# A 2-byte adjacency aggregation rewritten as one Strassen level, with its scalings on ScalarE and the repeat in the other arm of a branch

## The chip, the cores and the metric

The kernel runs on one core of one Trainium2 chip. TensorE multiplies matrices into PSUM, VectorE and ScalarE work element by element and read PSUM, GpSimd works element by element in SBUF and issues some DMAs, and SyncE (SP) issues the rest. Each engine runs its own instructions in order, and a semaphore wait holds all that stands behind it on that engine. The metric is device time in microseconds (us), the median of several runs.

## The reference

`x` has 3327 rows of 512, `adj` is a 3327 x 3327 matrix of zeros and ones (about 1% ones). Layer 0 is two attention layers with a residual and a norm; layer 1 is a binary graph layer, and its last two lines are what the change is about:

```python
def _gat_layer(x, W, adj):
    proj = x @ W
    Wh, Ws = jnp.split(proj, 2, axis=-1)
    a = jax.nn.softmax(Wh @ Ws.T, axis=-1) * adj
    return jax.nn.leaky_relu(a @ Wh + x, 0.01)
# layer 0
h = x
for l in range(2):
    h = _gat_layer(h, W_stack[l], adj)
x = _layernorm(x + h)
# layer 1: signs of the weights, positive signs of x
xw = (x > 0) @ sign(weight).T
x = _layernorm(x + relu(adj @ xw))
```

`xw` holds whole numbers of at most 512 in size, so `adj @ xw` can be multiplied with both operands in 2-byte floats without loss.

## The kernel before

Rows are cut into 26 tiles of 128 (the last has 127) and 13 groups of two tiles; a group is named g, a pair of tiles on the contracted side q or p. For each attention layer `project` makes the projections, and `attention` runs 169 steps (g, q). In a step TensorE makes scores some 30 steps ahead, VectorE and ScalarE make the softmax, `masked` multiplies by the adjacency pair (loaded by `load_adj`), `sums` makes Strassen's left sums on GpSimd, and `values` multiplies by one level of Strassen's scheme in fp32, with its right sums loaded as `ws`. The order of every engine inside a step is written by hand: each piece carries a position, and the pieces of a step are emitted sorted by it.

In the second layer two more things happen beside the steps. `halved` copies each adjacency pair to 2 bytes on GpSimd and stores it in DRAM (`adj_d`), and `exact` counts, on VectorE, the entries that the 2-byte copy changed. `finish` ends a group: residual, statistics (`mv`), sign, and the product `xw` (L781), which goes to DRAM as 2-byte numbers (`xw_d`) and is loaded again by `load_products`.

The aggregation then needs, for output tile t, 26 matmuls of 128 x 128 by 128 x 512 in 2-byte floats (`aggregate`, L896), one for each tile j. Adjacency comes in slabs of four tiles (`load_aggregate`, L883), seven slabs a group, into the ring of 33 slots called "s". The first 66 matmuls fill TensorE while group 12 finishes its attention; `finale` runs the others group by group. After a tile's 26 matmuls `norm_out` loads `h` (L115), standardizes it (L907), adds the rectified sum (L910), takes the moments (L912, L914), and scales (L916 on ScalarE, L917 and L919 on VectorE); the store goes out on GpSimd's queue. `finale` stands outside the hand-ordered part: there the framework's scheduler orders the instructions.

At the very end the count is reduced to one flag (L939 to L945), each engine loads it (L946), and a branch (L947) skips a repeat of the aggregation in fp32 unless an entry was not exact.

Of the kernel before, what the change touches and what calls it, by code (L numbers as in the profile page):

```python
# [9 lines left out]
F32 = mybir.dt.float32  # L10
# [9 lines left out]
P = 128  # L20
# [9 lines left out]
def kernel(  # L30
# [18 lines left out]
    def rows(t):  # L49
        return min(P, N - t * P)  # L50
# [360 lines left out]
    def attention(l, att):  # L411
# [199 lines left out]
        def halved(g, q):  # L611

            _, n = half_cols(g)
            at = adj[g, q]
            ah = att.tile([P, 2, HW], F16, tag="adj_h", bufs=2, name=f"ah_{g}_{q}")
            adj[g, q, "h"] = ah
            to = adj_d[g]
            if rows(2 * q + 1) == P:
                nc.gpsimd.tensor_copy(ah[:, :, :n], at[:, :, :n])
                nc.gpsimd.dma_start(out=to[:, 2 * q : 2 * q + 2, :n], in_=ah[:, :, :n])  # L620
                return
            for a in range(2):
                j = 2 * q + a
                r = rows(j)
                nc.gpsimd.tensor_copy(ah[:r, a, :n], at[:r, a, :n])
                load_rows(nc.gpsimd, to[:, j, :n], ah[:, a, :n], r)

        def exact(g, q):

            _, n = half_cols(g)  # L630
            at, ah = adj.pop((g, q)), adj.pop((g, q, "h"))
            junk = att.tile([P, 2, HW], U8, tag="junk", bufs=1, name=f"junk_{g}_{q}")
            i = g * NQ + q
            if rows(2 * q + 1) == P:
                nc.vector.scalar_tensor_tensor(
                    junk[:, :, :n], ah[:, :, :n], 1.0, at[:, :, :n], ALU.mult, ALU.not_equal,
                    accum_out=cnt[:, i : i + 1],
                )
                return
            both = small.tile([P, 2], F32, tag="both", name=f"both_{g}")  # L640
            nc.vector.memset(both, 0.0)
            for a in range(2):
                r = rows(2 * q + a)
                nc.vector.scalar_tensor_tensor(
                    junk[:r, a, :n], ah[:r, a, :n], 1.0, at[:r, a, :n],
                    ALU.mult, ALU.not_equal, accum_out=both[:r, a : a + 1],
                )
            nc.vector.reduce_sum(cnt[:, i : i + 1], both, axis=AX.X)

# [189 lines left out]
                do()  # L839
            return  # L840

        fill = [(0, j, i) for j in range(EARLY) for i in range(2)]
        fill += [(1, j, 0) for j in range(EARLY)]
        for n, do in zip((2, 8, 26, 4, 6, 6, 6, 4, 4), later):
            do()
            for g, j, i in fill[:n]:
                aggregate(g, j, i)
            fill = fill[n:]
        for g, j, i in fill:
            aggregate(g, j, i)  # L850


    JL = 4
    EARLY = NT - 4
    XH = NT // 2
    xw, xw_tiles, ah, po = {}, [], {}, {}

    def load_products(v):


        first = NQ * (NQ - 3), NQ * NQ - 16
        if v in first:
            xh = ops.tile([P, XH, D], F16, tag="gs", name=f"xw_{len(xw_tiles)}")
            xw_tiles.append(xh)
            for a in range(XH):
                xw[len(xw)] = xh[:, a]
        for t in range(2 * NQ - 2):
            g, i = divmod(t, 2)
            made = (g + 1) * NQ - 1 + (5, 9)[i]
            if v == max(made + 1, first[t // XH] + t % XH):  # L870
                nc.sync.dma_start(out=xw[t], in_=xw_d[t])
        g, j0 = divmod(v - first[1], -(-NT // JL))
        if 0 <= g < 2:
            load_aggregate(g, [j0 * JL])

    def load_aggregate(g, parts=range(0, NT, JL)):
        _, n = half_cols(g)
        for j0 in parts:
            t = slot([P, JL, HW], F16, f"ahl_{g}_{j0}")
            js = range(j0, min(NT, j0 + JL))  # L880
            full = [j for j in js if rows(j) == P]
            if full:
                nc.sync.dma_start(  # L883
                    out=t[:, : len(full), :n], in_=adj_d[g, :, j0 : j0 + len(full), :n]
                )
            for j in js:
                if rows(j) < P:
                    load_rows(nc.sync, t[:, j - j0, :n], adj_d[g, :, j, :n], rows(j))
                ah[g, j] = t[:, j - j0]

    def aggregate(g, j, i):
        t = 2 * g + i
        if j == 0:
            pool, tag = (ps_ch, "ch") if (g, i) < (1, 1) else (ps_acc, "acc")
            po[t] = pool.tile([P, D], F32, tag=tag, name=f"agg_{t}")
        nc.tensor.matmul(  # L896
            po[t][: rows(t)], ah[g, j][: rows(j), i * P : i * P + rows(t)],
            xw[j][: rows(j)], start=(j == 0), stop=(j == NT - 1),
        )

    def norm_out(t, po, tag):
        r = rows(t)
        span = slice(t * P, t * P + r)
        h = ring.tile([P, D], F32, tag="h", name=f"ho{tag}_{t}")
        load_rows(nc.sync, h, h_d[span, :], r)
        h = h[:r]
        nc.vector.tensor_scalar(  # L907
            h, h, mv[:r, t, 0:1], rstd[:r, t : t + 1], ALU.subtract, ALU.mult
        )
        nc.vector.scalar_tensor_tensor(h, po[:r], 0.0, h, ALU.max, ALU.add)  # L910
        st = small.tile([P, 6], F32, tag="bn", name=f"bo{tag}_{t}")
        nc.vector.bn_stats(st[:r], h)  # L912
        m2 = small.tile([P, 2], F32, tag="mv2", name=f"mo{tag}_{t}")
        nc.vector.bn_aggr(m2[:r], st[:r])  # L914
        rs = small.tile([P, 1], F32, tag="rs", name=f"rs{tag}_{t}")
        nc.scalar.activation(rs[:r], m2[:r, 1:2], AF.Sqrt, bias=eps[:r])  # L916
        nc.vector.reciprocal(rs[:r], rs[:r])  # L917
        o = ring.tile([P, D], F32, tag="xr", name=f"out{tag}_{t}")
        nc.vector.tensor_scalar(  # L919
            o[:r], h, m2[:r, 0:1], rs[:r], ALU.subtract, ALU.mult  # L920
        )
        load_rows(nc.gpsimd, out[span, :], o, r)

    def finale():
        nc.scalar.activation(rstd, mv[:, :, 1], AF.Sqrt, bias=eps)
        nc.vector.reciprocal(rstd, rstd)
        for g in range(NQ):
            if g > 1:
                load_aggregate(g)
            for j in range(NT):  # L930
                for i in range(2):
                    if j >= EARLY or (g, i) >= (1, 1):
                        aggregate(g, j, i)
            for i in range(2):
                norm_out(2 * g + i, po[2 * g + i], "")


        bad = small.tile([P, 1], F32, tag="bad", name="bad")
        nc.vector.reduce_max(bad, cnt, axis=AX.X)  # L939
        pb = ps_tr.tile([1, P], F32, tag="tr", name="pbad")  # L940
        nc.tensor.transpose(pb, bad, ident)
        flag = small.tile([1, 1], F32, tag="flag", name="flag")
        nc.vector.reduce_max(flag, pb, axis=AX.X)
        flag_i = small.tile([1, 1], I32, tag="flag_i", name="flag_i")
        nc.vector.tensor_copy(flag_i, flag)  # L945
        inexact = nc.values_load(flag_i[0:1, 0:1], min_val=0, max_val=2 * CW)  # L946
        with tc.If(inexact > 0):  # L947
            for t in range(NT):
                r = rows(t)
                pf = ps_acc.tile([P, D], F32, tag="acc", name=f"aggf_{t}")  # L950
                for j in range(NT):
                    at = slot([P, P], F32, f"af_{t}_{j}")
                    load_rows(
                        nc.sync, at[:, :r],
                        adjT[j * P : j * P + rows(j), t * P : t * P + r], rows(j),
                    )
                    xf = slot([P, D], F32, f"xwf_{t}_{j}")
                    nc.vector.tensor_copy(xf[: rows(j)], xw[j][: rows(j)])
                    nc.tensor.matmul(
                        pf[:r], at[: rows(j), :r], xf[: rows(j)],  # L960
                        start=(j == 0), stop=(j == NT - 1),
                    )
                norm_out(t, pf, "f")

    for l in range(L):
        with tc.tile_pool(name=f"pre{l}", bufs=1, reuse_waits="tile") as pre:
            with tc.manual_schedule():
                project(l, pre)
        with tc.tile_pool(name=f"att{l}", bufs=2, reuse_waits="tile") as att:
            with tc.manual_schedule():  # L970
                attention(l, att)
            if l == L - 1:
                finale()


# [30 lines left out]
```

## Time and profile before

| what | value |
|---|---|
| time, median of 3 runs | 2721.83 us (2717.41 to 2726.82) |
| the profiled execution: time / span | 2719.29 us / 2717.4 us |
| TensorE, VectorE, ScalarE, GpSimd busy | 98%, 69%, 24%, 48% of the span |
| attention ends, aggregation alone from | about 2555 us |
| last aggregation matmul ends | about 2703 us |
| aggregation matmuls | 676 |
| DMA | 639.54 MB, mean 235 GB/s |

The times are of one profiled execution, from its first to its last instruction; the program's own time is a little longer than the span. A busy TensorE is not TensorE at its peak, since matmuls overlap; the distance between starts says what one costs. L numbers are lines of the kernel before.

### The profile page before, as it was taken

The numbers are of one execution on the slowest core, as the hardware profiler recorded it, in microseconds if no ns is written. First come the engines' busy times: TensorE is split into PE (matmuls) and PEld (weight loads), VectorE is DVE, ScalarE is ACT, GpSimd is POOL, SyncE is SP. The second block draws the span as 40 slices with busy tenths as digits, with TensorE's granted clock in tenths as the row PEclk, the third lists the DMA queues.
The fourth block names the chain that finished last, engine by engine and source line by source line (L and its number), as shares of the span: only waits on it lengthen the run. The fifth ranks groups of instructions, "written<-read, shape, count | busy, mean of one in ns | idle before, by whom it ended". The sixth has DMA issues, their size and how long they took to land.

```text
span 2717.4 us, 38059 instructions
## 1 busy us (share of the span) xinstructions
PE 2651.7 (98%) x12409; PEld 2233.5 (82%) x12409; DVE 1877.1 (69%) x3511; ACT 665.2 (24%) x1571; POOL 1313.6 (48%) x2170
## 2 busy tenths in 40 slices
PE   9999999999999999998999999999999999998997
PEld 6888888888888888876888888888888888877543
DVE  5654777777777777786664667777677777778543
ACT  2323222222222222211332322222222222222100
POOL 2450455555555555775452154545545455566401
PEclk9999999999999999999999999999999999999999
DMA  5765777676777767776665667777777777687882
GB/s 191 258 208 161 237 233 257 226 260 233 257 238 235 260 227 240 254 260 220 235 206 178 206 224 261 239 248 255 238 252 237 275 236 242 235 274 255 286 284 92
DMA packets 280817, 639.54 MB, mean 235 GB/s; under 512 B 35921, under 2 KB 128735, under 8 KB 279078
## 3 DMA queue, kind: packets, MB, share of 16 engines
q1 hardware_dynamic: 244038, 527.32, 58.7%
q0 software_dynamic: 36576, 109.73, 11.0%
q8 instruction: 102, 1.67, 0.2%
q14 instruction: 101, 0.83, 0.1%
HBM read 527.22 MB, written 109.69 MB: 234 GB/s over the span
## 4 chain that ended last, share of the span: by engine, by line
PE 85%; issue 6%; DMA 4%; POOL 3%; DVE 2%; SPq 0%; ACT 0%; POOLq 0%; DVEq 0%; ACTq 0%
PE acc L682 34%; PE pZ L441 19%; PE pY L441 10%; PE pX L441 5%; PE pZ_wh L309 3%; PE pD L441 3%; PE pZ_g L363 3%; DMA ws<-ws_d 2%; PE pY_wh L309 2%; PE pY_g L363 2%; PE pm L273 1%; PE pxw L781 1%; PE pxt L221 1%; PE pX_wh L309 1%; PE pX_g L363 1%
## 5 line engine op out<-in xcount | busy, mean ns | idle before, releaser
L441 PE MATMUL pZ<-gs,xs 128*128 128x256 f32 x2496 | 635.8, 379 | 0.0
L441 PEld LDWEIGHTS pZ<-gs,xs 128*128 128x128 f32 x2496 | 473.6, 190 | 64.8 <-ACT u L458 0.3
L655 POOL TENSOR_TENSOR as<-s 128x128 f32<-128x128 f32 x338 | 168.4, 498 | 734.1 <-DVE s L600 577.1
L682 PE MATMUL acc<-ws,s 128*128 128x256 f32 x1352 | 404.3, 381 | 0.0
L682 PE MATMUL acc<-ws,as 128*128 128x256 f32 x1352 | 352.7, 382 | 30.0 <-DMA ws<-ws_d 17.4
L682 PE MATMUL acc<-wh,s 128*128 128x256 f32 x1352 | 356.9, 380 | 1.7 <-DVE h L706 1.7
L441 PE MATMUL pY<-gs,xs 128*128 128x256 f32 x1248 | 320.3, 379 | 0.0
L511 DVE TENSOR_TENSOR top<-top,s 128x512 f32<-128x512 f32 x312 | 252.7, 810 | 97.8 <-ACT s L493 58.2
L682 PEld LDWEIGHTS acc<-ws,as 128*128 128x128 f32 x1352 | 253.6, 190 | 75.0 <-POOL as L657 12.8
L682 PEld LDWEIGHTS acc<-wh,s 128*128 128x128 f32 x1352 | 258.0, 191 | 37.5 <-DVE h L706 2.1
L682 PEld LDWEIGHTS acc<-ws,s 128*128 128x128 f32 x1352 | 257.3, 191 | 35.1 <-DVE h L714 0.2
L582 DVE TENSOR_TENSOR s<-s,off 128x512 f32<-128x512 f32 x338 | 273.0, 808 | 0.1
L483 DVE TENSOR_TENSOR s<-p,u 128x256 f32<-128x256 f32 x156 | 67.5, 433 | 286.2 <-ACT u L458 285.3
L441 PEld LDWEIGHTS pY<-gs,xs 128*128 128x128 f32 x1248 | 237.0, 190 | 32.3
L585 ACT ACTIVATE s<-s 128x512 f32<-128x512 f32 x338 | 213.7, 632 | 201.5 <-DVE s L582 200.5
L593 DVE TENSOR_TENSOR total<-total,s 128x512 f32<-128x512 f32 x312 | 259.3, 831 | 0.8 <-ACT s L585 0.8
L657 POOL TENSOR_TENSOR as<-s 128x128 f32<-128x128 f32 x338 | 236.5, 700 | 26.5
L600 DVE TENSOR_TENSOR s<-s,adj 128x512 f32<-128x512 f32 (+1 forms) x312 | 226.1, 725 | 5.7
L458 ACT COPY u<-pZ 128x256 f32<-128x256 f32 x312 | 116.4, 373 | 459.9 <-PE pZ L441 459.9
L656 POOL TENSOR_TENSOR s<-s 128x128 f32<-128x128 f32 x338 | 215.2, 637 | 26.5
L658 POOL TENSOR_TENSOR as<-s,as 128x128 f32<-128x128 f32 x338 | 210.5, 623 | 26.5
L682 PE MATMUL acc<-wh,as 128*128 128x256 f32 x676 | 205.8, 386 | 0.0
(185 smaller groups left out, 3501.1 us busy)
## 6 DMA issues: line engine op xcount, KB each, us to landing
ws<-ws_d SPq DMA_DIRECT2D x338, 512.0 KB, 3.9
xs<-xs_d SPq DMA_DIRECT2D x182, 512.0 KB, 5.9
adj<-in_adjT_dram SPq DMA_DIRECT2D x288, 256.0 KB, 4.4
xs<-xs_d SPq DMA_DIRECT2D x156, 384.0 KB, 6.3
gs_d<-gsp POOLq DMA_DIRECT2D x88, 256.0 KB, 3.2
gs<-gs_d SPq DMA_DIRECT2D x12, 1792.0 KB, 11.0
adj_d<-ah POOLq DMA_DIRECT2D x144, 128.0 KB, 4.4
ahl<-adj_d SPq DMA_DIRECT2D x72, 256.0 KB, 4.4
```

The costliest lines, as they stand in the source:

```text
L309: nc.tensor.matmul(bank, of[LEFT[i]][:, k], wr[RIGHT[i]][:, k], start=(start and k == 0), stop=(k == 1), skip_group_check=True,)
L441: nc.tensor.matmul(ch[bank], xs[c, q, a][:, k], gs[c][:, b, k], start=(start and k == 0), stop=(k == 1), skip_group_check=True,)
L511: nc.vector.tensor_tensor(top[i], top[i], t, ALU.max)
L582: nc.vector.tensor_tensor(s, s, off[g].to_broadcast([P, 2, HW]), ALU.subtract)
L585: nc.scalar.activation(sc[g, q], sc[g, q], AF.Exp)
L593: nc.vector.tensor_tensor(total[g], total[g], sc[g, q], ALU.add)
L600: nc.vector.tensor_tensor(s[:, :, :n], s[:, :, :n], at[:, :, :n], ALU.mult)
L655: nc.gpsimd.tensor_tensor(s3, a11, a21, ALU.subtract)
L656: nc.gpsimd.tensor_tensor(a21, a21, a22, ALU.add)
L657: nc.gpsimd.tensor_tensor(s2, a21, a11, ALU.subtract)
L658: nc.gpsimd.tensor_tensor(s4, a12, s2, ALU.subtract)
L682: nc.tensor.matmul(acc[g][i // 2][:, i % 2], a[i], b[i], start=(q == 0 and i % 2 == 0), stop=(q == NQ - 1), skip_group_check=True,)
```

## The change

- **Aggregation.** A group's two output tiles are made together by one level of Strassen's scheme: seven products of 128 x 128 by 128 x 256 for each pair p of 13, so 91 matmuls a group in place of 52 twice as wide. Products lie two to a PSUM bank, (0, 1), (2, 3), (4, 5), (6), and the banks are worked one after the other, each over all 13 pairs. Groups alternate between two sets of four banks.
- **Sums.** `product_sums` makes four right sums for each pair on VectorE (44 of 52 operations in the last row of the attention), in the space of `wh`. `adjacency_sums` makes four left sums a slab: s1 and s2 on VectorE, s3 on GpSimd, s4 on VectorE for groups 0 and 1 and on GpSimd from group 2 on. Each slab and its sums take a slot of the ring "s". The padded last tile is filled with zeros by memsets on GpSimd.
- **Loads.** The slabs of groups 0 and 1 are loaded every second step of the last 27 or so steps, not every step of the last 16. Those of group g+1 are loaded while group g runs.
- **Output.** `take_out` adds the products from PSUM; `standard` standardizes `h` on ScalarE in two operations; `moments` as before; `scaled` scales on ScalarE in two operations, on VectorE in the last group. The store goes out on SP's queue. `h` now lies in the four buffers "adj", two a group.
- **Order.** `finale` stands in the hand-ordered part; all its pieces have positions.
- **Exactness.** `exact` compares `adj` with (`adj` > 0) and no longer reads the 2-byte copy. The flag is made in group 11; the branch's first arm holds the last group's output, the other arm the repeat.

```diff
@@ exact
-                    junk[:, :, :n], ah[:, :, :n], 1.0, at[:, :, :n], ALU.mult, ALU.not_equal,
+                    junk[:, :, :n], at[:, :, :n], 0.0, at[:, :, :n], ALU.is_gt, ALU.not_equal,
...
@@ end of attention
-        fill = [(0, j, i) for j in range(EARLY) for i in range(2)]
-        fill += [(1, j, 0) for j in range(EARLY)]
-        for n, do in zip((2, 8, 26, 4, 6, 6, 6, 4, 4), later):
+        fill = [
+            (g, b, p, i) for g in range(2) for b in range(3) for p in range(EARLY)
+            for i in BANKS[b]
+        ]
+        for n, do in zip((4, 16, 48, 8, 12, 12, 12, 8, 8), later):
...
+        finale(att)
-    EARLY = NT - 4
+    NS = -(-NT // JL)
+    EARLY = NQ - 2
+    BANKS = (0, 1), (2, 3), (4, 5), (6,)
...
@@ load_products
+        p = v - NQ * (NQ - 1) - 2
+        if 0 <= p < EARLY:
+            product_sums(p)
+        n, odd = divmod(v - NQ * NQ + 4 * NS - 1, 2)
+        if odd:
+            return
+        if 0 <= n < 2 * NS:
+            load_aggregate(*divmod(n, NS))
+        if 0 <= n - 1 < 2 * NS - 1:
+            adjacency_sums(*divmod(n - 1, NS))
+
+    def product_sums(p):
+        x1, x2 = xw[2 * p], xw[2 * p + 1]
+        xt[p] = wh[p].bitcast(F16).rearrange("p a n -> p (a n)")[:, : 4 * HD].rearrange(
+            "p (i n) -> p i n", i=4
+        )
+        right_sums(x1[:, :HD], x1[:, HD:], x2[:, :HD], x2[:, HD:], *(xt[p][:, i] for i in range(4)))
...
+    def adjacency_sums(g, s):
+        n = min(JL, NT - s * JL) // 2
+        a = ah[g, s].rearrange("p (b k) (i c) -> p b k i c", k=2, i=2)[:, :n]
+        a11, a21, a12, a22 = (a[:, :, k, i] for k in range(2) for i in range(2))
+        t = slot([P, 4, 2, P], F16, f"asm_{g}_{s}")
+        s1, s2, s3, s4 = (t[:, i, :n] for i in range(4))
+        nc.gpsimd.tensor_tensor(s3, a11, a21, ALU.subtract)
+        nc.vector.tensor_tensor(s1, a21, a22, ALU.add)
+        nc.vector.tensor_tensor(s2, s1, a11, ALU.subtract)
+        (nc.vector if g < 2 else nc.gpsimd).tensor_tensor(s4, a12, s2, ALU.subtract)
...
+    def aggregate(g, b, p, i):
+        if p == 0 and i == BANKS[b][0]:
+            pool, tag = (ps_acc, "acc") if g % 2 else (ps_ch, "ch") if b < 3 else (ps_tr, "tr")
+            po[g, b] = pool.tile([P, 2, HD], F32, tag=tag, name=f"agg_{g}_{b}")
...
+        nc.tensor.matmul(
+            po[g, b][:, i % 2], asm[g, p][i], of[i],
+            start=(p == 0 and i % 2 == 0), stop=(p == NQ - 1), skip_group_check=True,
+        )
...
@@ finale (norm_out and the old finale are removed)
+        def load_h(g):
+            for t in half_tiles(g):
+                h = h_of[t] = att.tile([P, D], F32, tag="adj", bufs=4, name=f"ho_{t}")
+                load_rows(nc.sync, h, h_d[t * P : t * P + rows(t), :], rows(t))
+
+        def standard(t):
...
+            nc.scalar.activation(h, h, AF.Identity, bias=nmean[:r, t : t + 1])
+            nc.scalar.activation(h, h, AF.Identity, scale=rstd[:r, t : t + 1])
...
+        def scaled(t, fast):
...
+            nc.vector.reciprocal(rs[:r, 0:1], rs[:r, 0:1])
+            if fast:
...
+            else:
+                nc.vector.tensor_scalar(rs[:r, 1:2], m2[:r, 0:1], -1.0, None, ALU.mult)
+                nc.scalar.activation(h, h, AF.Identity, bias=rs[:r, 1:2])
+                nc.scalar.activation(h, h, AF.Identity, scale=rs[:r, 0:1])
+            load_rows(nc.sync, out[t * P : t * P + r, :], h, r)
...
+        for g in range(NQ):
...
+            done = {b: (n + 1) / len(todo) for n, (b, p, i) in enumerate(todo)}
+            t1, t2 = half_tiles(g)
+            if 1 <= g and g + 1 < NQ:
+                for s in range(NS):
+                    work += [
+                        (-0.1 + s / NS, lambda s=s: load_aggregate(g + 1, s)),
+                        (0.04 + s / NS, lambda s=s: adjacency_sums(g + 1, s)),
+                    ]
+            if g + 1 < NQ:
+                work.append((0.5, lambda: load_h(g + 1)))
+            work += [(0.1, lambda: standard(t1)), (0.3, lambda: standard(t2))]
+            if g == NQ - 2:
+                work.append((0.95, check))
+            if g < NQ - 1:
+                for b in range(3):
+                    work.append((done[b] + 0.02, lambda b=b: take_out(g, b)))
+                work += [(0.98, lambda: moments(t1, c_of[g][0]))]
+            if g > 0:
+                u1, u2 = half_tiles(g - 1)
+                work += [
+                    (0.001, lambda: take_out(g - 1, 3)), (0.05, lambda: scaled(u1, False)),
+                    (0.08, lambda: moments(u2, c_of[g - 1][1])),
+                    (0.2, lambda: scaled(u2, False)),
+                ]
+            for _, do in sorted(work, key=lambda e: e[0]):
+                do()
         inexact = nc.values_load(flag_i[0:1, 0:1], min_val=0, max_val=2 * CW)
-        with tc.If(inexact > 0):
+        with tc.If(inexact < 1) as cmp:
...
+            moments(t1, c_of[g0][0])
+            scaled(t1, True)
+            take_out(g0, 3)
...
+        with cmp.Else():
```

`take_out(g, b)` is the attention's function of that name with the banks' products: for bank 0 a ScalarE copy of the first product and one VectorE sum, for bank 1 two sums, for bank 2 three, for bank 3 one.

## The prediction

> **What bounds the kernel now.** The page comes first: TensorE is busy nearly everywhere.
>
> ```profile
> span 2717.4 us, 38059 instructions
> PE 2651.7 (98%) x12409; PEld 2233.5 (82%) x12409; DVE 1877.1 (69%) x3511; ACT 665.2 (24%) x1571; POOL 1313.6 (48%) x2170
> ```
>
> 98% is an average, so I read the stage that the change rewrites, the aggregation, in the table by stretches (busy us per engine, then clock, DMA share, GB/s):
>
> ```profile
> 2510.00:2520.00 10.00, 7.83 (x32) 6.32 (x31) 8.85 (x15) 1.75 (x3) 7.92 (x12) 0.83 0.85 300
> ...
> 2555.00:2703.00 148.00, 147.85 (x691) 68.00 (x689) 70.17 (x162) 9.70 (x30) 14.96 (x27) 1.00 0.67 219
> 2703.00:2717.40 14.40, 0.00 (x0) 0.00 (x0) 3.79 (x12) 0.54 (x2) 1.61 (x3) 0.65 0.13 41
> ```
>
> From 2555 to 2703 TensorE never stops; VectorE works half the time, ScalarE 7%, GpSimd 10%. The chain of waits shows one group of 256 rows leaving every 11.2 us (2672.86 to 2684.08), which is 52 matmuls:
>
> ```profile
> 2672.86 0.54 POOL out_dram L115
> ...
> 2684.08 0.54 POOL out_dram L115
> ```
>
> So one matmul costs 11.22/52 = 0.2157 us. The groups then give the prices of operations like the new ones (mean ns after the busy time):
>
> ```profile
> L896 PE MATMUL agg<-xw,ahl 128*128 128x512 f16 x625 | 141.6, 379 | 0.0
> L585 ACT ACTIVATE s<-s 128x512 f32<-128x512 f32 x338 | 213.7, 632 | 201.5 <-DVE s L582 200.5
> L916 ACT ACTIVATE rs<-mo,eps 128x1 f32<-128x1 f32 x25 | 6.2, 288 | 128.5 <-DVE mo L914 128.5
> L714 DVE TENSOR_TENSOR h<-acc,h 128x256 f32<-128x256 f32 x26 | 10.8, 415 | 0.0
> L721 POOL TENSOR_TENSOR total<-total 128x256 f32<-128x256 f32 x26 | 19.8, 761 | 0.0
> ```
>
> and the DMA issues of 2640 to 2703, when the queues are light, the time to landing (last number, us):
>
> ```profile
> out_dram<-out POOLq DMA_DIRECT2D x11, 256.0 KB, 4.0
> ho<-h_d SPq DMA_DIRECT2D x9, 256.0 KB, 3.2
> ahl<-adj_d SPq DMA_DIRECT2D x6, 255.0 KB, 3.7
> ```
>
> Last, the timeline of the end: VectorE's last scaling starts at 2706.34 and takes 0.55; from its end to the end of the span pass 10.5 us (last stores, branch, end).
>
> **What the Trainium skill says.** (1) "TensorE: Matmul & The Clock Gate", Back-to-back issue gap: N/2.4 + 2.5 ns for a warm stream. N = 512 gives 215.8, the trace 215.7; so 256 columns cost 109 ns. Each new matmul loads its own weights; in the trace four transposes at L771, each with its own load, start 0.22 us before the next matmul, 55 ns apiece, so loads hide. (2) "VectorE: DVE Perf Modes", perf-mode tier table: two-input operations on 2-byte data run two elements a cycle. No row here shows one; with the page's (cycles + 151)/0.96 a 256-element sum is an estimated 290 ns, against 424 unpaired, near the 415 above. (3) "GPSIMD Engine Reference", Performance versus the Vector engine: about 2.6 cycles an element for two inputs. The trace's best 128- and 256-element sums, 442 and 722 ns, give 2.2 ns an element, which is that. (4) "ScalarE: Activation LUTs", What ACT_TABLE_LOAD costs: a per-partition scale or bias adds 93 ns. The trace has 632 without and 288 for one element with; so Identity on 512 elements costs an estimated 706 ns. The same page puts identity in every table set, so no table switches.
>
> **The change, part by part.**
>
> *Matmuls.* 676 x 0.2157 = 145.8 us become 13 x 13 x 7 = 1183 x 0.109 = 129.2: a gain of 16.6 us, if TensorE stays the bound. A group costs 91 x 0.109 = 9.9 us.
>
> *The count of inexact entries* reads fp32 twice instead of a 2-byte copy: same elements, same form, 690 ns either way. VectorE no longer waits for GpSimd's cast (28 us in all, hidden under TensorE except in the last row of the attention). Zero.
>
> *Sums during the last attention row (2497 to 2555).* VectorE gets 44 product sums (about 0.3 us each, 13 us) and some 20 adjacency sums (6 us) on 42 busy of 57; GpSimd 7 sums and memsets (7 us) on 43. Against that the 14 adjacency loads are spread over 27 steps instead of 14, in a stage where DMA is at 0.85 to 0.99 and TensorE waits for ws. I take +4 us (bounds -3, +10): TensorE there is fed by VectorE and GpSimd, so nothing hides an overload.
>
> *Start.* The fill hides the last group's finishing as before (132 half matmuls for 66). xw of the last tile, at 2570.8 before, comes at 2574.8; then VectorE runs four product sums (1.2), the last adjacency sums (0.7), the take-outs of group 0 (2.3), its moments with one more take-out and sum (5.4 less overlap 1.0): the second moments of group 0 end at about 2583.4. Call such an end M.
>
> *The ring of one group.* Engines run in order, and the changed order closes a ring from M (moments of t2, group g-1) to the next M:
> - ScalarE: square root, standard(t1 of g), then scaled(t2 of g-1): 0.3 + 2 x 0.7 + 2 x 0.7, with overlaps 3.05 us.
> - SP: the store of t2 now stands on SP, not GpSimd. Landing: 3.4 us (SP's 256 KB transfers show 3.2 to 3.7; the old store 4.0).
> - SP: load_h(g+1) takes over that buffer ("adj" has 4, two a group), so it waits for the landing, and behind it on SP stand slabs 5 and 6 of group g+1. 0.4 us to issue, 3.5 to land: slab 5 is there at M + 10.4.
> - VectorE reaches the sums of slab 5 at M + 7.5 and waits. Behind them stand take_out(2), the sums of slab 6, moments t1, take_out(3), the sums of slab 0 of g+2, two reciprocals, moments t2: 2 x 0.3, 3 x 0.36, 0.5, 1.65, 0.36, 0.6, 0.3, 1.65, with hand-overs and GpSimd's contention 6.2 us.
>
> Sum 16.6 us a group, against 9.9 of matmuls and 11.2 before. Eleven such turns (groups 1 to 11) take 182.6 us. TensorE waits some 5 us a turn for slabs 5 and 6. GpSimd's 14 sums (12 x 0.72 + 2 x 0.45 = 9.5, with contention up to 1.7 times that) fit inside.
>
> *End.* The check stands before the last take-outs (+0.9 in group 11, gone from the end). From the last M: ScalarE's queue and the branch 5.4, take-outs, two moments and scalings 8.0, then as before 10 us (the jump over the other arm replaces the old one).
>
> Sum: 2583.4 + 182.6 + 0.9 + 13.4 + 10.0 = 2790.3 us of span, against 2717.4. The profiled execution took 2719.3 (span + 1.9), the median of the runs is 2721.8 (2.5 above it). Carried over: 2795.
>
> **Rivals.**
> - *Ring without the store.* If slabs 5 and 6 land in time (the two landings together under 4 us instead of 6.9), the ring closes over ScalarE alone: M, 3.05, standard(t2), copy of p1 at 4.65, then VectorE's nine microseconds: 13.6 a group, 2762. For it: no SP store is in the trace, so its landing is the least known term. Against it: transfers that land in under 2 us hardly occur there, and an instruction that waits does hold SP (from 2400 to 2555 its queue stood 68 us behind loads of ws that waited for TensorE).
> - *TensorE stays the bound (faster).* If sums and stores keep ahead, TensorE ends 16.6 - 4 earlier and the end is 1.5 shorter: 2703.5, carried over 2708. It decides where a turn takes about 10 us (2790.3 - 72.9 spread over 11 turns). VectorE alone has 10 us of work a group (14 adjacency sums 3.7, take-outs 2.6, moments 3.3, small ones 0.5), so it needs every wait gone. In the trace's favour: VectorE is half idle here now.
> - *A slower ring.* Sums unpaired (424 ns: +0.8), landings as in the busy stage (4.1 and 4.3: +1.5), GpSimd's contention (its 128-element sums double from 0.45 to 0.79 beside VectorE): 19.3 a turn, 2824. GpSimd alone would bind beyond 16.6, at 1.7 times its bare time.
> - *No effect*: losses of the row and gains of the matmuls cancel: needs a turn near 10.5.
>
> **How the numbers follow.** The ring with the store 0.64, without it 0.15, the slower one 0.08, the faster case 0.09, no change 0.04. Slower 0.87, same 0.04, faster 0.09; 0.3% (8 us) is about what three runs can tell. The likeliest time is 2795; its own range is 2770 to 2820 (turns of 15 to 18.3 us, the row -3 to +10). Down to 2750 and up to 2824 the range takes in the ring without the store and part of the slower one.
>
> **What would show it.** Right: TensorE's busy share from 2600 on falls to about 0.65, with gaps once per group and a lower clock; groups leave every 16 to 17 us; SP waits for the landing of out_dram at load_h; VectorE's longest waits are for slab 5 (ahl). The first 2440 us are as before. Wrong: groups every 10 to 11 us with TensorE full; a VectorE or GpSimd that is busy throughout (then the sums are the price, not the waits); table loads on ScalarE; a last attention row that has grown by more than 10 us. The weakest terms are the two landings, which no SP store of before shows, and the 290 ns of a 2-byte sum.

## The result

The changed kernel takes 2838.86 us (median of 4 runs, 2837.61 to 2839.85), the kernel before 2719.62 us beside it: ratio 1.0435, 95% interval 1.0416 to 1.0454. Slower, as forecast, but by 119 us where 73 were forecast, and outside the range. The page of the changed kernel, then its table by stretches (busy us per engine, then clock, DMA share, GB/s):

```profile
span 2838.1 us, 39982 instructions
PE 2677.3 (94%) x12891; PEld 2298.8 (81%) x12916; DVE 1972.7 (70%) x3825; ACT 739.4 (26%) x1684; POOL 1437.3 (51%) x2332
```

```profile
2525.00:2550.00 25.00, 21.09 (x90) 16.62 (x91) 24.37 (x53) 4.13 (x8) 16.47 (x26) 0.93 0.79 254
...
2600.00:2650.00 50.00, 31.38 (x205) 22.50 (x206) 27.21 (x78) 13.74 (x24) 26.06 (x41) 0.70 0.49 156
...
2750.00:2800.00 50.00, 27.73 (x193) 20.61 (x191) 24.03 (x67) 14.39 (x26) 22.69 (x37) 0.74 0.38 121
```

From 2600 on, where TensorE was full before, it works 63% of the time at first, 73 and 68% in the two stretches left out, and 55% in the last. No engine is full in its place: VectorE and GpSimd work half the time, ScalarE a third. So the time is in waits. The first line is the last row of the attention: there VectorE is full (24.37 of 25 us). The same 25 us in the kernel before:

```profile
2525.00:2550.00 25.00, 20.65 (x94) 16.01 (x93) 17.56 (x33) 3.58 (x6) 20.41 (x32) 1.00 0.89 303
```

The timeline of VectorE gives the length of a turn. M is the end of such a line, the moments of a group's second tile:

```profile
2709.84 0.18 DVE L1000 BATCH_NORM_AGGREGATE mo<-bo 128x2 f32<-128x6 f32 x1
...
2728.22 0.18 DVE L1000 BATCH_NORM_AGGREGATE mo<-bo 128x2 f32<-128x6 f32 x1
```

From the one line to the other a turn takes 18.4 us. The eleven turns are 20.4, 18.8, 18.3, 18.7, 19.0, 19.7, 18.4, 18.6, 18.6, 21.0 and 32.2 us; the first M is at 2595.2, the last at 2818.8. Against the forecast of 2790.3 for the span:

| stretch | forecast | measured | difference |
|---|---|---|---|
| to the first M | 2583.4 | 2595.2 | +11.8 |
| nine ordinary turns | 9 x 16.6 | 9 x 18.9 | +21 |
| last two turns | 2 x 16.6 | 21.0 + 32.2 | +20 |
| flag (measured inside the last turn) | 0.9 | | -0.9 |
| from the last M to the end | 23.4 | 19.3 | -4.1 |

The sum is +48, which is 2838.1. Who waits for whom in the ordinary turns, from 2610 to 2750 (engine and line, what released it: us in all, times, longest)?

```profile
PE agg L939 <- DMA ahl<-adj_d: 43.3, 26, 3.8
DVE asm L925 <- DMA ahl<-adj_d: 30.1, 21, 3.7
...
DVE c L981 <- ACT ap L980: 27.4, 7, 3.9
```

VectorE waits for slabs of the adjacency (`ahl`) and for ScalarE's copy of the first product (`ap`, called p1 here); TensorE waits for slabs. VectorE and ScalarE wait for no matmul there, and GpSimd only twice (4.2 us in all), so TensorE's lower clock (0.70 to 0.79) is not what sets the turn. What holds up SP, which issues the loads? Its own waits in the same stretch:

```profile
SPq L115 <- ACT rs L1002: 42.2, 8, 5.3
SPq L115 <- POOL ahl L906: 37.7, 7, 5.7
...
SPq L115 <- DMA out_dram<-ho: 1.3, 6, 0.4
```

The landing of the store, a term of 3.4 us in the forecast's ring, is the last line: 1.3 us in seven turns. In its place stands L906, a memset on GpSimd that fills the padded tile of a group's last slab. It holds SP 5.4 us a time. The timelines of GpSimd and of VectorE in one turn show why, and what it costs:

```profile
2720.76 0.67 POOL L927 TENSOR_TENSOR asm<-ahl,asm 128x256 f16<-128x256 f16 x1 [0.22 <-DVE asm L926]
2721.37 0.31 POOL L906 MEMSET ahl<- 128x256 f16 x1
```

```profile
2719.72 0.29 DVE L925 TENSOR_TENSOR asm<-ahl 128x256 f16<-128x256 f16 x1 [0.69 <-DMA ahl<-adj_d]
...
2723.87 0.22 DVE L925 TENSOR_TENSOR asm<-ahl 128x128 f16<-128x128 f16 x1 [2.19 <-DMA ahl<-adj_d]
```

The memset takes 0.31 us, but it is written after the fourth sum of slab 5 in GpSimd's queue, so it can't start before slab 5 has landed and been summed. The load of slab 6's padded tile waits for the memset, and two slabs of the group after stand behind it on SP. VectorE then waits 2.19 us in front of slab 6. In the last turn every slab has such a memset, one column wide, since group 12 has 255 columns. GpSimd there:

```profile
2789.65 0.75 POOL L924 TENSOR_TENSOR asm<-ahl 128x256 f16<-128x256 f16 x1 [3.43 <-DMA ahl<-adj_d]
2790.62 0.67 POOL L927 TENSOR_TENSOR asm<-ahl,asm 128x256 f16<-128x256 f16 x1 [0.22 <-DVE asm L926]
2791.23 0.12 POOL L908 MEMSET ahl<- 128x4 f16 x1
2794.45 0.75 POOL L924 TENSOR_TENSOR asm<-ahl 128x256 f16<-128x256 f16 x1 [3.10 <-DMA ahl<-adj_d]
```

Load, sums, memset, next load: 4.8 us a slab, one after the other. That reading makes SP's queue and memsets of 0.1 to 0.3 us responsible for some 40 us. Whether it holds, only runs can tell.

### The profile page after: what moved, and what is told of

Same layout as the page of the kernel before. It is cut to its first block, busy times and chain, and to the rows that moved or that the text cites. A ratio compares the mean times of both kernels' runs of the same rounds, so it can differ in the third digit from the quotient of the medians.

```text
span 2838.1 us, 39982 instructions
## 1 busy us (share of the span) xinstructions
PE 2677.3 (94%) x12891; PEld 2298.8 (81%) x12916; DVE 1972.7 (70%) x3825; ACT 739.4 (26%) x1684; POOL 1437.3 (51%) x2332
## 4 chain that ended last, share of the span: by engine, by line
PE 82%; DMA 5%; DVE 5%; POOL 3%; issue 2%; ACT 1%; SPq 0%; POOLq 0%; DVEq 0%; ACTq 0%
PE acc L681 32%; PE pZ L441 19%; PE pY L441 9%; PE pX L441 5%; PE pZ_wh L309 3%; PE pD L441 3%; PE pZ_g L363 3%; DMA ahl<-adj_d 3%; PE agg L939 2%; DMA ws<-ws_d 2%; PE pY_wh L309 2%; PE pY_g L363 1%; PE pxt L221 1%; PE pX_wh L309 1%; PE pm L273 1%
## 5 line engine op out<-in xcount | busy, mean ns | idle before, releaser
L654 POOL TENSOR_TENSOR as<-s 128x128 f32<-128x128 f32 x338 | 168.1, 497 | 731.9 <-DVE s L600 319.2
L681 PE MATMUL acc<-ws,as 128*128 128x256 f32 x1352 | 356.9, 386 | 28.4 <-DMA ws<-ws_d 18.8
L511 DVE TENSOR_TENSOR top<-top,s 128x512 f32<-128x512 f32 x312 | 246.1, 789 | 110.3 <-ACT s L493 65.3
L655 POOL TENSOR_TENSOR s<-s 128x128 f32<-128x128 f32 x338 | 233.9, 692 | 26.5
L656 POOL TENSOR_TENSOR as<-s 128x128 f32<-128x128 f32 x338 | 221.2, 654 | 26.5
L657 POOL TENSOR_TENSOR as<-s,as 128x128 f32<-128x128 f32 x338 | 216.5, 641 | 26.5
## 6 DMA issues: line engine op xcount, KB each, us to landing
gs<-gs_d SPq DMA_DIRECT2D x12, 1792.0 KB, 11.1
```

The source lines that it names most:

```text
L511: nc.vector.tensor_tensor(top[i], top[i], t, ALU.max)
L654: nc.gpsimd.tensor_tensor(s3, a11, a21, ALU.subtract)
L655: nc.gpsimd.tensor_tensor(a21, a21, a22, ALU.add)
L656: nc.gpsimd.tensor_tensor(s2, a21, a11, ALU.subtract)
L657: nc.gpsimd.tensor_tensor(s4, a12, s2, ALU.subtract)
L681: nc.tensor.matmul(acc[g][i // 2][:, i % 2], a[i], b[i], start=(q == 0 and i % 2 == 0), stop=(q == NQ - 1), skip_group_check=True,)
```

## The experiments

Twelve kernels were timed beside the kernel before. Line numbers differ a little between them. "Mean turn" is the mean of the eleven. First M and mean turn are of one profiled execution each, whose time can lie some us off the median (pads 4.6 above it, pfo_nosums 5.9).

| kernel | median us | ratio to before (95%) | first M | mean turn |
|---|---|---|---|---|
| changed kernel | 2838.9 | 1.0435 (1.0416 to 1.0454) | 2595.2 | 20.3 |
| pads | 2797.6 | 1.0289 (1.0271 to 1.0306) | 2592.6 | 17.1 |
| first | 2785.0 | 1.0248 (1.0231 to 1.0265) | 2592.9 | 15.3 |
| pads_first | 2780.4 | 1.0228 (1.0211 to 1.0245) | 2592.1 | 15.1 |
| pads_bufs | 2801.8 | 1.0302 (1.0285 to 1.0320) | 2595.0 | 16.9 |
| order_alone | 2848.6 | 1.0478 (1.0461 to 1.0496) | 2598.5 | 21.1 |
| scale_dve | 2841.1 | 1.0453 (1.0436 to 1.0470) | 2595.0 | 20.2 |
| pf_order | 2754.6 | 1.0130 (1.0113 to 1.0147) | 2591.4 | 12.9 |
| pfo_s4 | 2762.3 | 1.0152 (1.0130 to 1.0173) | 2593.3 | 13.4 |
| pf_noxt | 2774.5 | 1.0206 (1.0189 to 1.0223) | 2588.0 | 15.1 |
| pf_noadj | 2730.6 | 1.0048 (1.0031 to 1.0066) | 2586.5 | 10.8 |
| pfo_nosums | 2718.5 | 0.9996 (0.9987 to 1.0005) | 2585.8 | 10.3 |
| exact_alone | 2723.2 | 1.0019 (1.0008 to 1.0030) | | |

### pads: the memsets out of the loads' way

```diff
@@ halved
+                if n < HW:
+                    nc.gpsimd.memset(ah[:, :, n:], 0.0)
                 nc.gpsimd.tensor_copy(ah[:, :, :n], at[:, :, :n])
-                nc.gpsimd.dma_start(out=to[:, 2 * q : 2 * q + 2, :n], in_=ah[:, :, :n])
+                nc.gpsimd.dma_start(out=to[:, 2 * q : 2 * q + 2], in_=ah)
...
@@ load_aggregate
-        if len(full) < len(js):
-            nc.gpsimd.memset(t[:, len(full) : len(js)], 0.0)
-        if n < HW:
-            nc.gpsimd.memset(t[:, : len(js), n:], 0.0)
...
+        nc.sync.dma_start(out=t[:, : len(js)], in_=adj_d[g, :, j0 : j0 + len(js)])
```

> Edit: the padding of the halved adjacency (column 255 of the last group, row 127 of the last tile) is zeroed before it is stored, during the attention, so the slab loads of the aggregation bring it along; the memsets on GpSimd and the extra load issues of the last slab are gone. Theory A (SP, in order, is held at the last slab until GpSimd has worked off its sums and reaches the memset): the nine ordinary turns fall from 18.9 us to 16.7, close to the 16.6 of the forecast, the last two from 21.0 and 32.3 to the same length; 9 x 2.2 + 4.3 + 15.6 = 40 us less, 2799 us. Theory B (the time goes to VectorE's and GpSimd's own work on the sums, and the memset only stands where SP would wait anyway): ordinary turns stay at 18 to 19, only the last two become ordinary, 16 us less, 2823 us.

Measured: 2797.6 us, 41 less. Ordinary turns are 16.5 to 18.7 us, the last two 16.7 and 17.6. Theory A holds, and with it the size: a wait of SP for GpSimd, not GpSimd's work (it has all its sums still), cost 41 of the 119 us. Two smaller things went with the memsets, and no run separates them: the extra loads for the padded tile (two a group, 0.75 us on SP in the turn above), and the last group's rows of 255 columns, whose slabs landed no later than others (2.9 us against 3.0). SP's waits in the same stretch no longer contain a memset:

```profile
SPq L115 <- ACT rs L993: 87.1, 9, 10.1
...
SPq L115 <- DMA out_dram<-ho: 1.1, 5, 0.2
```

What is left is SP's wait for ScalarE, whose scaled tile it is to store; the landing of the store is again nearly nothing.

### pads_bufs: is the landing of the store in the ring?

```diff
@@ load_h
+            if g % 2:
+                two = att.tile([P, 4, HD], F32, tag="ws", name=f"ho2_{g}")
             for t in half_tiles(g):
...
+                if g % 2:
+                    h = h_of[t] = two[:, 2 * i : 2 * i + 2].rearrange("p a n -> p (a n)")
```

> On top of pads: the h tiles of every second group lie in the buffers of ws, which is idle by then, so a load of h never waits for the landing of a store two groups back. The forecast had that landing in its ring with 3.4 us a turn: if so, turns fall from 16.8 to about 13.4, 2760 us. From the trace of pads SP stands only 1.1 to 1.5 us between the store and the load of h, and VectorE waits 0.9 us for slab 5: turns 15.9, 2788 us. If the landing is hidden: no change, 2798 us.

Measured: 2801.8 us, not less than pads. The landing is hidden: SP reaches the load of h 4.5 to 4.9 us after M with it and 4.5 to 4.6 without, because it issues two slabs between the store (M + 3.1) and that load. The third case of the expectation came true; my reading of the trace of pads, 0.9 us a turn, was also wrong.

### first and pads_first: the slabs ahead of the stores

```diff
@@ finale
-                        (-0.1 + s / NS, lambda s=s: load_aggregate(g + 1, s)),
+                        (-1.0 + 0.1 * s, lambda s=s: load_aggregate(g + 1, s)),
```

> Edit: within a group, the seven slab loads of the next group are put at the head of the list, ahead of the stores and of the loads of h on SP; memsets stay. Theory A (slabs 5 and 6 are late because SP stands at the stores, the loads of h and the memsets): VectorE does not wait for slabs any more, the ring closes over ScalarE and VectorE alone, 13.6 us a turn as worked out in the forecast's first rival: first M at 2595, 11 x 13.6, 19 us of end, 2765 us. Theory B (the sums themselves are the price): turns stay near 18, 2825 to 2839 us.

> Both edits: padding zeroed before it is stored, and the slab loads at the head of each group. Theory A: as with the slabs first alone, and up to 10 us less, since SP waits for no memset at all: 2755 to 2765 us. Theory B: 16 us below the changed kernel, 2823 us.

Measured: 2785.0 and 2780.4 us. Most of A's gain is there: VectorE waits for slabs no more (but once in first, 2.3 us), nearly all turns are 15.1 us, and with the slabs first the memsets cost little more (4.6 us, with one turn of 17.8 us, the last but one). But 13.6 us was too low. VectorE's longest wait in pads_first, from the table of waits, and ScalarE's timeline of one turn (M at 2666.63):

```profile
DVE c L972 <- ACT ap L971: 39.1, 10, 3.9
```

```profile
2666.67 0.29 ACT L993 ACTIVATE rs<-mo,eps 128x1 f32<-128x1 f32 x1
2666.87 0.71 ACT L958 ACTIVATE ho<-ho,nmean 128x512 f32<-128x512 f32 x1
2667.61 0.72 ACT L959 ACTIVATE ho<-ho,rstd 128x512 f32<-128x512 f32 x1
2668.24 0.71 ACT L1007 ACTIVATE ho<-ho,rs 128x512 f32<-128x512 f32 x1
2668.98 0.72 ACT L1008 ACTIVATE ho<-ho,rs 128x512 f32<-128x512 f32 x1
2669.61 0.71 ACT L958 ACTIVATE ho<-ho,nmean 128x512 f32<-128x512 f32 x1
2670.34 0.72 ACT L959 ACTIVATE ho<-ho,rstd 128x512 f32<-128x512 f32 x1
2670.97 0.35 ACT L971 COPY ap<-agg 128x256 f32<-128x256 f32 x1
```

The copy of p1, which VectorE needs to take the first bank out, stands behind the square root and six scalings: it ends at M + 4.7, as the forecast's first rival had it (4.65). From there VectorE needs 10.4 us to the next M, not 9: sums of 2-byte data that take 0.28 to 0.29 us alone take 0.59 to 0.66 beside GpSimd's. So the ring over ScalarE exists, behind the one over SP.

### pf_order: ScalarE's order

```diff
@@ finale
-            work += [(0.1, lambda: standard(t1)), (0.3, lambda: standard(t2))]
+            work += [(0.1, lambda: standard(t1)), (0.45, lambda: standard(t2))]
...
-                    (0.2, lambda: scaled(u2, False)),
+                    (0.32, lambda: scaled(u2, False)),
```

> On top of pads_first: the scalings of the second tile and the standardisation of the second tile stand behind the copy of p1 on ScalarE instead of ahead of it (positions 0.32 and 0.45 of a group, for 0.20 and 0.30). Theory (each turn VectorE stands 3.9 us in front of that copy, which is behind six scalings): the wait falls to about 0.9, 12.1 us a turn, 2747 us. Rival (VectorE's and GpSimd's own work, 10.8 and 9.5 us a turn with contention, takes up what is freed): 13.5 or more, 2763 us. If the wait is off the path: 2780 us.

Measured: 2754.6 us, 25.8 less; turns are 12.9 us. That is about midway between the theory (2747) and its rival (2763), and both have a share in it: VectorE's wait for the copy of p1 fell from 3.9 to 1.3 us a turn, and the sums took up part of what was freed. The table by stretches:

```profile
2600.00:2650.00 50.00, 45.27 (x365) 36.32 (x364) 43.15 (x122) 25.62 (x44) 38.08 (x56) 0.92 0.65 217
```

VectorE works 86% of the time and TensorE 91%. The waits are mostly gone and the work of the sums stands out. This is the fastest version with all of the computation that was run, and it is still 1.3% slower than the kernel before.

### order_alone: the same edit on the changed kernel

The two lines of pf_order, with memsets and slab loads where the changed kernel has them.

> On the changed kernel itself: only ScalarE's order (scalings and standardisation of the second tile behind the copy of p1), with memsets and slab loads left where they are. Theory (the slabs end last in the changed kernel's turn, the copy of p1 earlier): freed VectorE only waits longer for slab 5, and the store goes out no earlier; no gain, 2830 to 2845 us. Rival (each wait adds to the turn): the 2.2 us a turn that the same edit gave with the slabs ahead, 2815 us.

Measured: 2848.6 us, 10 more. No gain, as the theory said, but a loss just beyond what it allowed: the store of the second tile goes out at M + 4.1 instead of M + 3.1, so the slabs behind it come 1 us later, and the first nine turns are 19.7 us instead of 18.9. (3.3 of the 10 us lie ahead of the first M, which the edit hardly touches; the profiled execution was 4 us above the median.) VectorE's wait for slabs from 2610 to 2750 grew from 30.1 to 50.9 us. An edit that gives 2.2 us a turn once SP is free takes 0.8 while SP is not. It shows that SP's ring ended last, and that the store's place on SP, not its landing, is in it.

### scale_dve: the scalings of the outputs back on VectorE

```diff
-                    (0.001, lambda: take_out(g - 1, 3)), (0.05, lambda: scaled(u1, False)),
+                    (0.001, lambda: take_out(g - 1, 3)), (0.05, lambda: scaled(u1, True)),
...
-                    (0.2, lambda: scaled(u2, False)),
+                    (0.2, lambda: scaled(u2, True)),
```

> On the changed kernel itself: the scalings of the outputs back on VectorE, in one operation each; the standardisations stay on ScalarE. Theory: VectorE gets 0.8 us a turn, but the store of the second tile goes out about 1.3 us after M instead of 3.1, and with it the load of h and slabs 5 and 6 behind it: some 1 to 1.5 us less a turn, 2825 us. Rival (VectorE's work is the price): 0.8 us more a turn, 2848 us.

Measured: 2841.1 us, no change. Both were wrong; the trace shows two effects of opposite sign and like size. VectorE's timeline (M at 2709.29):

```profile
2707.20 1.15 DVE L996 SCALAR_TENSOR_TENSOR ho<-c,ho 128x512 f32<-128x512 f32 x1
...
2709.91 0.92 DVE L1011 TENSOR_SCALAR ho<-ho,mo,rs 128x512 f32<-128x512 f32 x1
```

The store does go out earlier, at M + 1.6 instead of M + 3.1. But the scaling takes 0.92 us here, against 0.546 in the kernel before, where GpSimd had next to nothing to do; and of each two L996 one takes 1.15 instead of 0.69. In the stretch before M that is 1.4 us more on VectorE, against the 1.5 us by which the store is earlier. Having the scalings on ScalarE neither cost nor gained anything in this kernel.

### pfo_s4: how much of the sums' time is disturbance

```diff
-        (nc.vector if g < 2 else nc.gpsimd).tensor_tensor(s4, a12, s2, ALU.subtract)
+        nc.vector.tensor_tensor(s4, a12, s2, ALU.subtract)
```

> On top of pf_order: the fourth adjacency sum (s4) of every slab on VectorE instead of GpSimd. VectorE gets 1.9 us of work a turn at the undisturbed 0.28 us. If the two engines disturb each other (s2 takes 0.29 us alone and 0.51 on average in pf_order), VectorE gets some 1.7 back and turns stay at 12.5 to 13, 2755 us. If VectorE's operations simply take what they take: 14.6 us a turn, 2776 us.

Measured: 2762.3 us, 7.7 more, or 0.7 a turn: nearer to the disturbance (0) than to the bare work (21 us). The groups from 2610 to 2730, in pf_order and then in pfo_s4 (busy us, mean ns of one):

```profile
L917 DVE TENSOR_TENSOR asm<-asm,ahl 128x256 f16<-128x256 f16 x56 | 28.2, 503 | 1.9
L916 DVE TENSOR_TENSOR asm<-ahl 128x256 f16<-128x256 f16 x56 | 20.5, 366 | 0.7 <-DMA ahl<-adj_d 0.7
```

```profile
L917 DVE TENSOR_TENSOR asm<-asm,ahl 128x256 f16<-128x256 f16 x54 | 18.9, 350 | 1.9
L918 DVE TENSOR_TENSOR asm<-ahl,asm 128x256 f16<-128x256 f16 x54 | 18.8, 349 | 1.8
L916 DVE TENSOR_TENSOR asm<-ahl 128x256 f16<-128x256 f16 x54 | 17.6, 326 | 0.6 <-DMA ahl<-adj_d 0.4 <-issue 0.2
```

VectorE makes half as many sums again, but the second sum falls from 503 to 350 ns. GpSimd's help with the fourth sum is worth 0.7 us a turn, not 1.9. The Trainium skill gives a reason ("SBUF — State Buffer", Who interferes with whom): a VectorE operation with two SBUF inputs contends with a GpSimd operation that reads SBUF, and so does one in a two-port mode, where whichever issues first holds the shared ports for its whole duration and the other is blocked. The trace agrees for the sums. The scaling of scale_dve also grew beside GpSimd (0.546 to 0.92 us); in which mode it runs no run shows.

### pf_noxt, pf_noadj, pfo_nosums: leaving sums out

These three leave out sums and multiply raw quarters or blocks in their place, so they don't compute the product; the number of matmuls stays.

```diff
@@ load_products (pf_noxt; pfo_nosums in product_sums itself)
-            product_sums(p)
+            xt[p] = [x1[:, :HD], x1[:, HD:], x2[:, :HD], x2[:, HD:]]
@@ adjacency_sums (pf_noadj for g > 1 only; pfo_nosums for all)
+        for b in range(n):
+            asm[g, 2 * s + b] = [e[:, b] for e in (a11, a12, a21, a22, a11, a12, a22)]
+        return
```

> On top of pads_first, left out: the 44 product sums that VectorE makes during the last row of the attention (raw quarters stand in, so part of the product is not computed). Theory (VectorE bounds that row, so its added 13 us of work come through nearly whole): the first M moves from 2592 to about 2581, 2769 us. Rival (the adjacency loads and GpSimd's sums hold the row up): at most 3 us, 2778 us.

> On top of pads_first, left out: all adjacency sums of groups 2 to 12 (raw blocks stand in, so part of the product is not computed); loads, matmuls, take-outs, moments, scalings and stores stay. If the ring over ScalarE and VectorE remains the bound: M, 4.9 us to the copy of p1, 6.2 us of take-outs and moments, 11.1 a turn, 2736 us. If only TensorE remains: 9.9 a turn, 2723 us. If the sums cost nothing on the path: 15.1 a turn, 2780 us.

> On top of pf_order, left out: every sum that the change adds, product sums and adjacency sums, in the last row of the attention and after it (raw blocks stand in, so the product is not computed). Forecast's faster rival (TensorE stays the bound): the row ends as before the change and the first M falls to about 2578, turns 10.0 us, 2578 + 110 + 20, 2709 us. If the ring over ScalarE stays at the 10.7 us of the run without adjacency sums: 2716 us. If the row does not come back (its adjacency loads are the price): 2720 us.

Measured: pf_noxt 2774.5 us, 5.9 less than pads_first, first M 4.1 us earlier (this execution was 1.5 us ahead already at 2380). That is about half of what the theory said, and more than its rival. VectorE stays full (19.5 of 20 us, twice, from 2510 to 2550) with the 44 sums gone: its other operations fill the time and take longer, a slab's three sums 0.48 to 0.54 us on average in place of 0.28 to 0.40, the count 0.97 in place of 0.76.

pf_noadj: 2730.6 us, turns of 10.8 where 11.1 and 9.9 were named. The ring over ScalarE is the bound once more (the copy of p1 is awaited 4.4 us a turn). It is still slower than before the change.

pfo_nosums: 2718.5 us, not the 2709 of the faster rival; of the two slower cases the trace supports the ring over ScalarE, since the last row did come back (see below). With every sum left out and both queues mended, the time is that of the kernel before (0.9996, 0.9987 to 1.0005). Its waits from 2600 to 2690:

```profile
DVE c L975 <- ACT ap L974: 35.9, 8, 5.6
ACT ho L961 <- DMA ho<-h_d: 19.1, 8, 3.5
```

Now h comes late, ScalarE standardizes it late, and the copy of p1 is behind that. TensorE works 98% from 2600 to 2650, but a turn is 10.3 us, not 9.9, and the first M is at 2585.8. So of the 16.6 us that the matmuls should save, nothing is left even in this form.

### exact_alone: the count on 4-byte data

The kernel before with the two lines of `exact` changed as in the diff above.

> The kernel before with one part of the change alone: the count of inexact entries reads the 4-byte tile twice instead of the 2-byte copy. Forecast: nothing, 2720 us within 0.3%. Rival: VectorE, freed of its waits for GpSimd's cast, or slowed by the wider operand, moves it by more than 8 us.

Measured: 2723.2 us, ratio 1.0019 (1.0008 to 1.0030): within 0.3%, as forecast, though not quite nothing: 5.2 us by the medians, which the changed kernel may carry too. The count runs in both attention layers, half of the pairs in each (156 operations, the first at 290 us). In the last row it takes 872 ns instead of 690, and its wait for GpSimd's cast (8.9 us ahead of six counts) is gone.

## Why the prediction was wrong

The direction was right, and so was the kind of mechanism: queues that run in order close a ring from M to M, and TensorE stands idle in it (55 to 73% busy after 2600, 65% forecast). But a link that the forecast's ring was built on, the landing of the store, is not in it, and another, the memset, was left out. The size was off in four steps.

**The ring of one group, its SP and VectorE parts.** The prediction went from the arrival of slab 5 to M in 6.2 us; in the turn above it is 8.7 (2719.72 to 2728.40). The terms that it lists for this stretch add up to 6.7 and not, hand-overs and contention included, to 6.2. The missing member is the memset ahead of slab 6, which makes VectorE wait 2.19 us: it was counted among GpSimd's work in the attention row, but not as an instruction that SP waits for and that GpSimd reaches late. With it away (pads), the kernel takes 2797.6 us against the 2795 forecast. That agreement is partly luck. The store's landing of 3.4 us that the ring contained is not in it (2.0 us, hidden: pads_bufs); VectorE's wait for the copy of p1, 3.9 us a turn, is, and stands where the forecast had a wait for slab 5 alone.

**Eleven equal turns.** The prediction multiplied one turn by eleven. The last group has 255 columns, so each of its seven slabs has a memset, and its loads go one by one: 20 us more than forecast in the last two turns, all but 1 us of it gone in pads (16.7 and 17.6). The one group that differs in shape had to be worked out by itself.

**The row of attention.** +4 us, bounds to +10; the last take-outs of that row came 13.9 us later. Part of that is older than the row: the statistics of tile 18 (`mv`), before any of the new loads and sums (the first load stands at 2436.9), are 3.6 us late in the profiled execution, here in the kernel before and in the changed one:

```profile
2378.45 0.18 DVE L763 BATCH_NORM_AGGREGATE mv<-bn 128x2 f32<-128x6 f32 x1
2382.04 0.18 DVE L762 BATCH_NORM_AGGREGATE mv<-bn 128x2 f32<-128x6 f32 x1
```

In the twelve other kernels the same statistics stand between 0.4 us earlier and 6.5 us later than before; exact_alone, which has only the new count, is 2.7 late. How much of this is the count and how much the spread of executions is not shown. From there to the last tile's statistics it takes 184.9 us in the kernel before, 195.7 in the changed one, 194.5 in pads_first, 190.4 without the product sums (pf_noxt) and 183.7 without any sum (pfo_nosums). So the row itself grew by about 10 us (10.8 in the changed kernel, 4 forecast), and all of it goes with the sums: the loads spread over more steps, which pfo_nosums keeps, cost nothing that can be seen. VectorE became the bound there, which the prediction named as a danger and then sized too low: it used 0.3 us a sum, and beside GpSimd most took 0.33 to 0.53 on average.

**End.** 4.1 us too long. Up to VectorE's last scaling, which ends at 2832.47, it was right: 13.6 us for 13.4. From there to the end of the span 5.6 us pass, where the forecast took over the 10 of the kernel before. The last stores land in 2.0 to 2.6 us on SP, and in 3.1 to 3.3 before; the rest lies behind the landing, and its cause stays open.

What held: 109 ns a matmul; 0.71 to 0.72 us a scaling on ScalarE (0.706 forecast); 0.28 to 0.29 us a 2-byte sum alone; 0.71 and 0.76 us on average for the two sums of a slab on GpSimd (0.72 forecast, before contention); the store at M + 3.1 (3.05 forecast); the first 2440 us, but for the 3.6 us above.

Of the rivals, "TensorE stays the bound" is refuted: not even pfo_nosums comes clearly under the kernel before. "Ring without the store" was right about what closes behind the SP ring, and 1.5 us short of its turn. "A slower ring" had the right direction, with GpSimd's contention as one of its causes, and the wrong main cause. "No effect" needed a turn near 10.5 us, which only pf_noadj (10.8) and pfo_nosums (10.3) come near.

The 119 us, taken apart by runs that build on one another: memsets 41, slab loads behind stores 17, ScalarE's order 26, sums 36; their total is 120. These are shares in this order of removal; order_alone shows that another order would divide them otherwise. The end point, pfo_nosums, has the cheaper matmuls and the new count, so what those save and cost is inside the 36.

## What to carry to other kernels

Follow every wait of an in-order queue to the engine that releases it, and then to what stands ahead of the releasing instruction on that engine: memsets of 0.1 to 0.3 us on the load path cost 41 us here because of their place, and zeros that were written once with the data cost nothing that could be seen. Work out the last, irregular group on its own before a turn is multiplied. And where a cheaper multiplication is bought with sums, price the sums beside what runs next to them: here the matmuls could have saved 17 us by the forecast's working, and the kernel as a whole lost that and 119 us more.

## What the hardware showed

- A 2-byte two-input sum of 256 elements on VectorE takes 0.28 to 0.29 us alone and up to 0.66 beside GpSimd's sums (pads_first); a 4-byte scaling by two per-partition values goes from 0.55 to 0.92 us (before, scale_dve). Operations that read PSUM for one input were not slowed (take-outs: 0.41 to 0.43 us in the changed kernel's last group, where GpSimd has no work, and 0.39 to 0.42 on average beside GpSimd in pf_order).
- A 256 KB store issued on SP landed in 2.0 us at the median of 2600 to 2800; on GpSimd's queue it took 4.0 before the change.
- TensorE's gaps are followed by slower matmuls. In pads_first, after 6 us in which TensorE works in short groups between waits, matmuls start 0.21 us apart up to 2666.5, then at the usual 0.11:

```profile
2665.82 0.42 PE L930 MATMUL agg<-xw,asm 128*128 128x256 f16 x1
2666.03 0.42 PE L930 MATMUL agg<-wh,asm 128*128 128x256 f16 x1
...
2666.76 0.27 PE L930 MATMUL agg<-wh,asm 128*128 128x256 f16 x1
2666.87 0.27 PE L930 MATMUL agg<-xw,asm 128*128 128x256 f16 x1
```

The Trainium skill ("TensorE: Matmul & The Clock Gate", Part 1: The HAM clock gate) has half the clock, 1.2 GHz, after an idle window of about 3.4 us; at that clock 256 columns take an estimated 213 ns, and the trace shows 0.21 us. The condition does not show here as the page puts it: the longest single wait ahead of the slow matmuls is 0.95 us. The granted clock was 0.83 from 2650 to 2700, in the changed kernel 0.70 to 0.79 from 2600 to 2750, in pfo_nosums 0.98 to 1.00.
